# Layer 2's experts: all tokens through all eight, or tokens sorted by expert into tiles of 128

## The chip, the cores and the metric

The kernel runs on one core of a Trainium2 chip. The core has a matrix engine (TensorE, here PE; its weight loads are PEld), a vector engine (VectorE, DVE), an activation engine (ScalarE, ACT), a general engine (GpSimd, POOL) and an engine that only issues transfers (SyncE, SP). They run side by side, each its own instructions in order, and wait for one another through semaphores. Transfers are carried out by 16 DMA engines. The metric is device microseconds for one execution of the whole program; lower is better.

## The reference

2048 tokens of 128 features (two batches of 1024) pass through four layers. Each layer is a feed-forward half step, an attention step and the same feed-forward half step again. The change concerns layer 2, whose feed-forward part is a mixture of eight experts of which each token uses the two with the highest router logits. Its input is the layer norm of x, and half of its output is added to x:

```python
logits = x_flat @ router_w
gate_vals, gate_idx = jax.lax.top_k(logits, TOP_K)             # TOP_K = 2
gate_w = jax.nn.softmax(gate_vals, axis=-1)
gates = jnp.zeros_like(logits).at[jnp.arange(N)[:, None], gate_idx].set(gate_w)
h = jax.nn.gelu(jnp.einsum('nd,edf->enf', x_flat, w1) + b1[:, None, :], approximate=False)
out = jnp.einsum('enf,efd->end', h, w2) + b2[:, None, :]
res = x_flat[None, :, :] + out
mu = jnp.mean(res, axis=-1, keepdims=True)
var = jnp.mean(jnp.square(res - mu), axis=-1, keepdims=True)
normed = (res - mu) * jax.lax.rsqrt(var + LN_EPS)
expert_out = normed * gamma[:, None, :] + beta[:, None, :]
y = jnp.einsum('end,ne->nd', expert_out, gates)
```

Here d = 128 and f = 512 per expert. The reference computes all eight experts for every token; six of the eight gates of a token are zero.

## The kernel before

Everything is float32. `c.x` holds the whole of x in SBUF, as 16 tiles of 128 tokens; four tiles make a chunk q of 512 tokens. The program is written as one stream. Only TensorE's order is taken as written (`manual_schedule` for PE); the other engines' instructions are ordered by a scheduler. Work that prepares the next stage is put into "threads": lists of pieces with `None` between them. `c.tick()` advances the first two threads up to their next `None`, and `c.need(key)` runs the rest of a thread at once. So a piece's place in TensorE's stream depends on how many ticks have passed.

Layer 2's feed-forward part (`l2_ffn`) runs `experts` (L270 to L330) over 4 chunks by 8 experts, 32 steps. In a step `hidden` makes the 512 hidden features of 512 tokens (four products of 512 columns, L284, with GELU and the bias on ACT, L292), then `output` does the step before: b2 by a product with ones (L299) and 16 products of 128 by 128 (L302). `combine` adds the input (L1166), takes the norm's statistics (L1168), and for each pair of experts works out scale and offset on DVE, applies them on ACT (L1183), multiplies by gamma on POOL (L1185) and adds to x on DVE (L1189). There is one tick per step. All of layer 2's weights, 2 MB for each of w1 and w2, are loaded once, before the first use (`l2_weights`).

The preparation of a chunk (`l2_ffn_prep`) is a norm (`norm_pieces`), a turn to feature order (L163), the router's logits (L218), the best two of eight (`top2`), the gates, and the beta term added to x (L267, L269). It takes eleven advances. Layer 1's feed-forward part, which comes before the first of layer 2, finishes chunk q at its iteration 4q + 8 of 21, with one tick per iteration. Layer 2's attention (`l2_attn`) comes between the two feed-forward parts; it handles eight groups (two batches by four head groups) of 16 steps with a tick each, and the last group's output is added to x after the last step. Its first projection (L1234 to L1263) is not interleaved with anything. After the second feed-forward part, layer 3 works on chunks that take 256 tokens from each batch (`places`), so its first needs tokens of both batches.

Of the kernel before, what the change touches and what calls it, by code (L numbers as in the profile page):

```python
# [29 lines left out]
class Ctx:  # L30
# [44 lines left out]
    def advance(self, thread):  # L75
        pieces = thread[1]
        while pieces:
            piece = pieces.popleft()
            if piece is None:
                break  # L80
            piece()
        if not pieces:
            self.threads.remove(thread)

# [89 lines left out]
def norm_pieces(c, r, q, scale=1.0, eps=1e-5, weight=None):  # L174


    def xs(j):
        return c.x[:, 4 * q + j, :]

    def apply():  # L180
        r["xn"] = c.act.tile([P, 4, P], F32, tag="xn", name="xn", bufs=4)
        norm_apply(c, r, xs, r["xn"])

    def turn():
        r["xT"] = by_feature(c, q, r["xn"], weight)

    return [partial(norm_stats, c, r, xs, (scale, eps)), None, None, apply, None, None, turn, None]


def top2(c, v, n):  # L190
# [5 lines left out]
    def largest(x, k):  # L196
        m = c.act.tile([P, 4], F32, tag=f"t2m{k}", name="t2m", bufs=2)
        eq = c.act.tile([P, 4, n], F32, tag=f"t2e{k}", name="t2e", bufs=2)
        f = c.act.tile([P, 4], F32, tag=f"t2f{k}", name="t2f", bufs=2)
        nc.vector.tensor_reduce(m, x, AX.X, ALU.max)  # L200
        nc.vector.tensor_tensor(eq, x, m.unsqueeze(2).to_broadcast([P, 4, n]), ALU.is_equal)
        nc.vector.tensor_tensor(eq, eq, rev, ALU.mult)
        nc.vector.tensor_reduce(f, eq, AX.X, ALU.max)
        nc.vector.tensor_tensor(eq, eq, f.unsqueeze(2).to_broadcast([P, 4, n]), ALU.is_equal)
        return m, eq
# [21 lines left out]
def pair_gates(c, lg, n):  # L227
# [3 lines left out]
    m1, o1, m2, o2 = top2(c, lg, n)  # L231
# [3 lines left out]
    def end():  # L235
        nc.vector.tensor_scalar(m2, m1, -0.25, 0.25, ALU.mult, ALU.add)
        nc.vector.tensor_scalar(m1, m1, 0.25, 0.25, ALU.mult, ALU.add)
        g = c.act.tile([P, 4, n], F32, tag="gates", name="gates", bufs=4)
        nc.vector.tensor_tensor(o1, o1, m1.unsqueeze(2).to_broadcast([P, 4, n]), ALU.mult)
        nc.vector.tensor_tensor(o2, o2, m2.unsqueeze(2).to_broadcast([P, 4, n]), ALU.mult)  # L240
        nc.vector.tensor_add(g, o1, o2)
        return g
# [4 lines left out]
def gate_pieces(c, r, q, router, n, rows, bias=None):  # L247
# [3 lines left out]
    def gates():  # L251
        r["end"] = pair_gates(c, router_logits(c, r, router, n, bias), n)
# [884 lines left out]
def l2_weights(c, pool):  # L1137
    w = {n: c.load(pool, f"l2f_{n}") for n in "router w1 b1 w2 beta".split()}
    w["gamma"] = c.load(pool, "l2f_gamma", rows=P)
    w["b2"] = pool.tile([3, 8 * P], BF16, tag="l2f_b2", name="l2f_b2")  # L1140
    with c.tc.tile_pool(name="parts", bufs=1) as work:
        three_parts(c, work, c.load(work, "l2f_b2", rows=3), w["b2"])
    for n in "wq wkv wo norm gq gk".split():
        w[n] = c.load(pool, f"l2a_{n}")
    return w


def l2_ffn_prep(c, w, rs, q):
    return norm_pieces(c, rs[q], q) + gate_pieces(c, rs[q], q, w["router"], 8, w["beta"])


def l2_ffn(c, w, rs, key, done):
    nc = c.nc
    with c.pool("l2f") as pool:
        two = {}

        def combine(q, e, py):


            k = e % 2  # L1160
            if k == 0:
                two["st"] = pool.tile([P, 4, 2, 6], F32, tag="rst", name="rst", bufs=3)
                two["todo"] = []
            st = two["st"]
            res = pool.tile([P, 4, P], F32, tag="res", name="res", bufs=5)
            nc.vector.tensor_add(res, py, rs[q]["xn"])  # L1166
            for j in range(4):
                nc.vector.bn_stats(st[:, j, k, :], res[:, j, :])  # L1168
            if k:
                mean, var, sc, off = (  # L1170
                    pool.tile([P, 8], F32, tag=n, name=n, bufs=3) for n in ("mean", "var", "sc", "off")
                )
                mean_var(c, mean, var, st)
                inv_sqrt(c, sc, var, 1.0, 1e-6)
                by_tile = lambda a: a.rearrange("p (j e) -> p j e", j=4)
                nc.vector.tensor_tensor(by_tile(sc), by_tile(sc), rs[q]["g"][:, :, e - 1 : e + 1], ALU.mult)
                nc.vector.scalar_tensor_tensor(off, mean, -1.0, sc, ALU.mult, ALU.mult)
                two["sc"], two["off"] = sc, off

            def finish(sc, off):  # L1180
                for j in range(4):
                    a = slice(2 * j + k, 2 * j + k + 1)
                    nc.scalar.activation(res[:, j, :], res[:, j, :], AF.Identity, scale=sc[:, a], bias=off[:, a])  # L1183
                gamma = w["gamma"][:, e * P : (e + 1) * P].unsqueeze(1).to_broadcast([P, 4, P])
                nc.gpsimd.tensor_tensor(res, res, gamma, ALU.mult)  # L1185

            def add():
                xs = c.x[:, 4 * q : 4 * q + 4, :]
                nc.vector.tensor_add(xs, xs, res)  # L1189
                if e == 7:  # L1190
                    done(q)

            two["todo"].append((finish, add))
            if k == 0:
                return []
            (f0, a0), (f1, a1) = two["todo"]
            sc, off = two["sc"], two["off"]
            return [partial(f0, sc, off), partial(f1, sc, off), a0, a1]

        experts(  # L1200
            c, pool, rs, w["w1"], w["w2"], w["b1"], AF.Gelu, 8, 4, combine, key, b2=w["b2"]
        )

# [7 lines left out]
def l2_attn(c, w, rs, key, done):  # L1211
    nc = c.nc
    with c.pool("l2a", 2) as pool:
# [6 lines left out]
        def project(b, f):  # L1220


            raw = pool.tile([P, TB, 2, 4, 64], F32, tag="raw", name="raw", bufs=1)
            tr = pool.tile([P, 2, 2, S], F32, tag="tr", name="tr")
            v = pool.tile([P, TB, 4, 64], F32, tag="v", name="v")
# [136 lines left out]
        for n, (b, f) in enumerate(groups):  # L1362
# [10 lines left out]
            for s in range(16):  # L1373
                k2 = s % 4
                if k2 == 0:
                    u = dict(p=s // 8, q=s // 4 % 2, v=v, aoT=aoT)
# [10 lines left out]
                c.tick()  # L1387
            outs = output(b, f, aoT)
        mix(*before)
        divide(ended)  # L1390
        for piece in outs:
# [26 lines left out]
def l3_ffn_prep(c, w, rs, work, q):  # L1418
# [13 lines left out]
    def apply_first():  # L1432
        r["xn"] = c.act.tile([P, 4, P], F32, tag="xn", name="xn", bufs=4)
# [208 lines left out]
def macaron(ctx: ExitStack, tc: tile.TileContext, dram: dict, out: bass.AP):  # L1642
# [35 lines left out]
    with ExitStack() as s1:  # L1678
# [16 lines left out]
        p2 = ctx.enter_context(c.pool("w2"))  # L1695
        w2 = l2_weights(c, p2)
        l1_ffn(c, w1, r[5], "f", follow("g", partial(l2_ffn_prep, c, w2, r[6])))
    r = [r[6]] + [chunks() for _ in range(4)]
    l2_ffn(c, w2, r[0], "g", follow("h", partial(l2_attn_prep, c, w2, r[1])))
    l2_attn(c, w2, r[1], "h", follow("i", partial(l2_ffn_prep, c, w2, r[2])))  # L1700
# [13 lines left out]
    l2_ffn(c, w2, r[2], "i", both_places)  # L1714
# [108 lines left out]
```

## Time and profile before

| | us |
|---|---|
| median of 3 runs (3280.83 to 3284.17) | 3281.82 |
| time of the profiled execution | 3285.2 |
| its span, first to last instruction | 3283.3 |
| layer 2's first feed-forward part, 1688 to 1940 in the span | 252 |
| layer 2's second feed-forward part, 2716 to 2963 | 247 |
| layer 2's attention with its start, 1940 to 2716 | 776 |

The profile's page gives busy time per engine, the busy share in 40 slices of the span, and the chain of work that ended last. The trace behind it can be asked for groups of instructions by line, for the timeline of a stretch, and for busy times of stretches. A product in float32 is recorded as two matmuls and two weight loads, so the counts are twice those of the code. In the timeline a row is several like instructions in a line: its start, its length, and how many.

### The profile page before, as it was taken

To read this page: it belongs to the slowest core of one execution; us is meant where nothing else is said; L and a number is where in the kernel's file an instruction comes from. 1 tells how busy PE (TensorE), PEld (TensorE's weight loads), DVE (VectorE), ACT (ScalarE), POOL (GpSimd) and SP (SyncE) were. 2 spreads that over 40 slices of the span, in tenths; PEclk is the share of its full clock that TensorE was granted. 3 is DMA by queue.
4 is the path that set the end of the run, shared out by engine and by line. 5 is a ranking of instruction groups with operands and counts; after the bars stand their busy time and mean duration, and the time that the engine had idled before them with its cause. 6 is when DMAs were issued, how large, how long until landed. Compare 5 with 4: busy or idle time off the path is not lost.

```text
span 3283.3 us, 44950 instructions
## 1 busy us (share of the span) xinstructions
PE 2980.2 (91%) x16080; PEld 1683.6 (51%) x16080; DVE 2121.4 (65%) x6759; ACT 1731.0 (53%) x3278; POOL 850.1 (26%) x769
## 2 busy tenths in 40 slices
PE   7999999999898788888789978999989999998989
PEld 5544545454564454444466653343334336666667
DVE  4665566656458588586565567777777755457774
ACT  3355454545333356565245536677756785555443
POOL 0011111111005354454321123544424431111100
PEclk9999999999898589999899998999989999998999
DMA  2000000000000000000100000000000001000000
GB/s 80 1 1 1 1 1 1 1 1 1 25 1 0 1 1 1 1 1 27 58 1 1 1 1 1 1 1 1 0 1 1 1 1 32 1 1 1 1 4 11
DMA packets 14215, 21.80 MB, mean 7 GB/s; under 512 B 5425, under 2 KB 11330, under 8 KB 13350
## 3 DMA queue, kind: packets, MB, share of 16 engines
q1 hardware_dynamic: 8546, 15.90, 1.5%
q10 hardware_dynamic: 5444, 3.01, 0.3%
q8 instruction: 127, 2.08, 0.3%
q14 instruction: 98, 0.80, 0.1%
HBM read 17.86 MB, written 1.05 MB: 6 GB/s over the span
## 4 chain that ended last, share of the span: by engine, by line
PE 74%; DVE 17%; ACT 4%; issue 2%; POOL 2%; DMA 0%; SPq 0%; ACTq 0%; DVEq 0%; POOLq 0%
PE py L302 13%; PE ph L284 12%; PE ps L1304 7%; PE po L1337 6%; PE ps L486 5%; PE po L528 4%; PE ptp L514 4%; PE pr L466 3%; PE po L1065 2%; PE pt L1053 2%; PE pqk L1238 1%; PE pr L556 1%; ACT pe L1031 1%; PE ps L1008 1%; DVE raw L1256 1%
## 5 line engine op out<-in xcount | busy, mean ns | idle before, releaser
L1311 ACT ACTIVATE pe<-ps 128x1024 f32<-128x1024 f32 x256 | 248.8, 1021 | 143.4 <-PE ps L1304 143.4
L1304 PE MATMUL ps<-tr 64*128 64x512 f32 x1024 | 268.4, 645 | 1.6 <-ACT pe L1311 1.6
L292 ACT ACTIVATE hT<-ph,l2f_b 128x512 f32<-128x512 f32 x256 | 162.1, 683 | 185.2 <-PE ph L284 185.2
L499 ACT ACTIVATE pe<-ps,nm 128x512 f32<-128x512 f32 (+3 forms) x384 | 219.6, 578 | 65.1 <-DVE nm L497 61.1
L1337 PE MATMUL po<-pe,v 128*64 128x512 f32 x1024 | 248.4, 606 | 2.3 <-ACT pe L1312 2.3
L1312 ACT ACTIVATE pe<-pe 128x2048 f32<-128x2048 f32 x128 | 244.8, 1913 | 4.1
L302 PE MATMUL py<-l2f_w,hT 128*128 128x128 f32 x2048 | 245.6, 278 | 0.0
L497 DVE TENSOR_REDUCE nm<-ps 128x2 f32<-128x256 f32 (+1 forms) x192 | 182.8, 952 | 95.6 <-PE ps L495 62.3
L302 PEld LDWEIGHTS py<-l2f_w,hT 128*128 128x128 f32 x2048 | 233.5, 192 | 14.5 <-issue 14.3
L347 DVE SCALAR_TENSOR_TENSOR x<-py,gates,x 128x128 f32<-128x128 f32 x448 | 132.7, 344 | 165.7 <-PE py L302 165.6
L284 PE MATMUL ph<-xT,l2f_w 128*128 128x512 f32 x512 | 230.7, 593 | 0.0
L96 ACT COPY pT<-ptp 128x512 f32<-128x512 f32 x192 | 92.0, 479 | 250.8 <-PE ptp L514 250.8
L1185 POOL TENSOR_TENSOR res<-res,l2f_gamma 128x512 f32<-128x512 f32 x64 | 91.0, 1421 | 447.5 <-ACT res L1183 439.5
L486 PE MATMUL ps<-kT,qT 64*128 64x512 f32 (+3 forms) x768 | 177.9, 539 | 30.0 <-ACT pe L499 11.3
L528 PE MATMUL po<-pT,v 128*64 128x512 f32 (+3 forms) x768 | 166.5, 512 | 0.0
L514 PE MATMUL ptp<-ident,pe 128*128 128x128 f32 x1152 | 162.2, 277 | 0.2 <-ACT rb L564 0.2
L1304 PEld LDWEIGHTS ps<-tr 64*128 64x128 f32 x1024 | 92.6, 195 | 129.1 <-issue 90.8
L1337 PEld LDWEIGHTS po<-pe,v 128*64 128x64 f32 x1024 | 62.3, 136 | 176.8 <-issue 150.6
L514 PEld LDWEIGHTS ptp<-ident,pe 128*128 128x128 f32 x1152 | 123.0, 141 | 51.5 <-issue 39.6
L302 PEld LDWEIGHTS py<-l3f_w,hT 128*128 128x128 f32 x1024 | 124.9, 193 | 31.6 <-issue 28.1
L284 PEld LDWEIGHTS ph<-xT,l2f_w 128*128 128x128 f32 x512 | 92.4, 190 | 92.7 <-issue 88.2
L1324 POOL TENSOR_TENSOR acp<-pe 128x1024 f32<-128x1024 f32 x32 | 76.4, 2387 | 220.7 <-ACT pe L1312 158.1
(374 smaller groups left out, 6372.4 us busy)
## 6 DMA issues: line engine op xcount, KB each, us to landing
l2f_w<-in_l2f_w SPq DMA_DIRECT2D x2, 2048.0 KB, 8.4
l3f_w<-in_l3f_w SPq DMA_DIRECT2D x2, 1024.0 KB, 4.9
l0f_W<-in_l0f_W SPq DMA_DIRECT2D x2, 768.0 KB, 4.9
l2a_wkv<-in_l2a_wkv SPq DMA_DIRECT2D x1, 1024.0 KB
x<-in_x SPq DMA_DIRECT2D x2, 256.0 KB
x<-in_x ACTq DMA_DIRECT2D x2, 256.0 KB, 4.5
l0a_wq<-in_l0a_wq SPq DMA_DIRECT2D x1, 512.0 KB
l0a_wqr<-in_l0a_wqr SPq DMA_DIRECT2D x1, 512.0 KB, 7.6
```

Source lines behind the costliest of these rows:

```text
L284: nc.tensor.matmul(ph[:, a, :], lhsT=w1[:, e, (k + a) * P : (k + a + 1) * P], rhs=rs[q]["xT"], start=True, stop=True)
L292: nc.scalar.activation(hT[:, k + a, :], ph[:, a, :], func, bias=bias)
L302: nc.tensor.matmul(py[:, j, :], lhsT=hT[:, k, j * P : (j + 1) * P], rhs=w2[:, e, k, :], start=(k == 0 and b2 is None), stop=(k == hc - 1), ...
L486: nc.tensor.matmul(ps[:, h, :W], lhsT=u["qT"][r, q0 : q0 + P], rhs=u["kT"][r, gk * 512 : gk * 512 + W], start=True, stop=not diag,)
L497: nc.vector.tensor_reduce(nm, ps[:, :, :W], AX.X, ALU.max, negate=True)
L499: nc.scalar.activation(u["pe", n][:, h, i, :W], ps[:, h, :W], AF.Exp, bias=nm[:, h : h + 1], accum_out=u["rs"][:, n, i, h : h + 1],)
L514: nc.tensor.transpose(pt[:, i * P : (i + 1) * P], u["pe", n][:, h, i, j * P : (j + 1) * P], c.ident)
L528: nc.tensor.matmul(u["po", n][r, lo * P :], lhsT=u["v"][:, BLOCKS[n][1] * 4 + j, cols], rhs=u["pT", n, j][h][:, lo * P :], start=(j == 0), ...
L1304: nc.tensor.matmul(ps[:, h, :], lhsT=tr[r, 1, p, k * P : (k + 1) * P], rhs=tr[r, 0, p, q * 512 : (q + 1) * 512], start=True, stop=True,)
L1311: nc.scalar.activation(pe[:, j], ps, AF.Tanh, scale=1.0 / 50.0)
L1312: nc.scalar.activation(pe, pe, AF.Exp, scale=50.0 * 0.125)
L1337: nc.tensor.matmul(u["po"][r, :], lhsT=u["v"][:, k, 2 * u["p"] + h, :], rhs=pe[:, j, h, :], start=(k == 0), stop=(k == TB - 1),)
```

## The change

Layer 2's feed-forward part no longer puts every token through every expert. Tokens are handled in two halves of 1024. For each half:

- The preparation also stores the normed rows in HBM (`xd`), and keeps the two one-hot rows of the chosen experts and the two gates.
- `l2_route` counts, by products of bf16 zeros and ones, how many earlier tokens chose the same expert. Each expert gets whole tiles of 128 places, at most 23 tiles for the 2048 pairs of token and expert. DVE works out each pair's place and each tile's expert; 16 more products invert the table, so that each place knows its token.
- `l2_ffn` runs over the 23 tiles, in groups of four. POOL gathers a tile's rows by an indirect DMA, each engine loads the tile's expert number into a register, SP loads that expert's w1 (256 KB), and the operands w2, b1, b2 and gamma are addressed by the register. There is a tick every second tile. The normed result, without the scale, is stored in HBM with its variance as a 129th column (`yd`).
- `l2_back` gathers, by indirect DMA, the two rows of each token, works out the scale from variance and gate, and adds both to x. It has five advances until x is done.

The first feed-forward part's halves are chunks (0,1) and (2,3), the second's (0,2) and (1,3). In `l2_attn` the last group handles its first 512 queries first and adds their output to x at steps 10 and 11, with two ticks per step from step 10. w2, gamma and b2 are loaded twice, the second time during that group. Buffers of `tr` and `v` lie in two pools, and `xn` has two buffers instead of four, with layer 3's in a pool of its own.

```diff
-def l2_ffn(c, w, rs, key, done):
...
+TILES = 23
+GROUPS = [range(i, min(i + 4, TILES)) for i in range(0, TILES, 4)]
...
+def l2_ffn_prep(c, w, keep, h, a):
...
+    def store():
+        nc.sync.dma_start(out=h["xd"][512 * a : 512 * a + 512, :].rearrange("(j p) d -> p j d", p=P), in_=r["xn"])
+
+    def end():
+        h["ready"] += 1
+        if h["ready"] == 2:
+            c.later(("route", h["name"]), l2_route(c, w, keep, h))
...
+    return [begin] + norm[:i] + [store] + norm[i:] + gates + [end]
...
+def l2_route(c, w, keep, h):
...
+        nc.tensor.matmul(ahead, lhsT=w["before"], rhs=m, start=True, stop=False, skip_group_check=True)
+        for t in range(TB - 1):
+            rhs = m[:, t : t + 1, :].to_broadcast([P, TB - 1 - t, 8])
+            nc.tensor.matmul(
+                ahead[:, t + 1 :, :], lhsT=c.ones16, rhs=rhs, start=False, stop=(t == TB - 2), skip_group_check=True
+            )
...
+    def one_hot_row():
+        r["a"] = tile_([16, P], "a", BF16)
+        nc.vector.tensor_tensor(r["a"], wide(w["iota"], 16), long(r["lo"], P), ALU.is_equal)
+
+    def invert():
+        pt = r["pt"] = c.bank("pt")[:, 0:48]
+        for k in range(16):
+            nc.tensor.matmul(
+                pt, lhsT=r["a"][:, k, :], rhs=r["b"][:, k].rearrange("p a i -> p (a i)"), start=(k == 0), stop=(k == 15)
+            )
...
+    return [pairs, None, count, None, places, None, one_hot, one_hot_row, None, None, invert, None, tokens, None]
...
+def l2_ffn(c, w, we, keep, halves, done):
...
+        def fetch(n):
+
+            h, g = groups[n]
+            xg[n] = keep.tile([P, 4, P], F32, tag="xg", name="xg", bufs=4)
+            for j, i in enumerate(g):
+                at = bass.IndirectOffsetOnAxis(ap=h["tok"][:, i : i + 1], axis=0)
+                nc.gpsimd.indirect_dma_start(xg[n][:, j, :], None, h["xd"], at)
+                e = expert[n, j] = nc.values_load(
+                    h["ex"][0:1, i : i + 1],
...
+                w1[n, j] = pool.tile([P, 512], F32, tag="w1", name="w1", bufs=8)
+                nc.sync.dma_start(
+                    out=w1[n, j], in_=c.dram["l2f_w1"][:, bass.ds(e, 1), :].rearrange("p e f -> p (e f)")
+                )
+
+        def ahead(n, force):
+
+            while fetched[0] < min(n + 3, len(groups)):
+                key = ("route", groups[fetched[0]][0]["name"])
+                if fetched[0] <= n and force:
+                    for a in range(2):
+                        c.need(("half", groups[fetched[0]][0]["qs"][a]))
+                    c.need(key)
+                elif groups[fetched[0]][0]["ready"] < 2 or c.waits(key):
+                    return
+                fetch(fetched[0])
+                fetched[0] += 1
...
+            for a in range(4):
+                nc.scalar.activation(
+                    hT[:, a, :], ph[:, a * P : (a + 1) * P], AF.Gelu, bias=w["b1"][:, bass.ds(e * 4 + a, 1)]
+                )
...
+            nc.vector.tensor_add(res[:, 0:m, :], py[:, 0:m, :], xg[n][:, 0:m, :])
+            for j in range(m):
+                nc.vector.bn_stats(st[:, j, 0, :], res[:, j, :])
+            mean_var(c, mean[:, 0:m], y[:, 0:m, P], st[:, 0:m])
...
+            nc.sync.dma_start(out=rows, in_=y[:, 0:m, :])
+            if g is GROUPS[-1]:
+                c.later(("back", h["name"]), l2_back(c, keep, h, done))
...
+        for k, (n, j) in enumerate((n, j) for n in range(len(groups)) for j in range(len(groups[n][1]))):
+            if j == 0:
+                if n == 0:
+                    ahead(0, True)
+                    turn(0)
+                if n + 1 < len(groups):
+                    ahead(n + 1, True)
+            if j == 2 and n + 1 < len(groups):
+                turn(n + 1)
+            now = (n, j, hidden(k, n, j))
+            if last is not None:
+                output(*last)
+            last = now
+            if k % 2:
+                c.tick()
...
+def l2_back(c, keep, h, done):
...
+                nc.gpsimd.indirect_dma_start(yg[a][:, k, j, :], None, h["yd"], at)
...
+    return [partial(fetch, 0), partial(fetch, 1), None, None, None, partial(add, 0), None, partial(add, 1), None]
...
+                if n + 1 == len(groups) and s >= 10:
+                    c.tick()
+                if n + 1 == len(groups) and s == 9:
+                    for d, piece in zip((10, 11), output(b, f, aoT)[0:2]):
+                        slots[d].append(piece)
...
+    h1, prep1 = halves(1, ((0, 1), (2, 3)))
+    h2, prep2 = halves(2, ((0, 2), (1, 3)))
```

## Prediction

> **What bounds the kernel now.** I read the page first: the busy shares, then the chain of waits, then the two stretches of the change alone.
>
> ```profile
> PE 2980.2 (91%) x16080; PEld 1683.6 (51%) x16080; DVE 2121.4 (65%) x6759; ACT 1731.0 (53%) x3278; POOL 850.1 (26%) x769
> ...
> PE 74%; DVE 17%; ACT 4%; issue 2%; POOL 2%; DMA 0%; SPq 0%; ACTq 0%; DVEq 0%; POOLq 0%
> PE py L302 13%; PE ph L284 12%; PE ps L1304 7%; PE po L1337 6%; PE ps L486 5%; PE po L528 4%; PE ptp L514 4%; PE pr L466 3%; PE po L1065 2%; PE pt L1053 2%; PE pqk L1238 1%; PE pr L556 1%; ACT pe L1031 1%; PE ps L1008 1%; DVE raw L1256 1%
> ```
>
> PE leads, and the two products of the experts head the chain. The stretches of layer 2's feed-forward parts (busy time per engine, granted clock, DMA share, GB/s):
>
> ```profile
> 1688.00:1940.00 252.00, 251.04 (x1388) 171.87 (x1386) 133.23 (x638) 137.52 (x266) 42.48 (x30) 1.00 0.00 1
> 2716.00:2963.00 247.00, 247.00 (x1368) 169.26 (x1368) 129.18 (x642) 136.14 (x267) 42.91 (x30) 1.00 0.01 4
> ```
>
> PE is never idle here, at full clock; every other engine is about half free. What leaves PE's stream shortens the program, until another engine or a wait takes over. One step in the timeline (start, length):
>
> ```profile
> 1700.63 3.60 PE L284 MATMUL ph<-xT,l2f_w 128*128 128x512 f32 x8
> ...
> 1704.16 0.39 PE L299 MATMUL py<-l2f_b,ones 3*128 3x512 bf16 x1
> ...
> 1704.48 3.84 PE L302 MATMUL py<-l2f_w,hT 128*128 128x128 f32 x32
> ```
>
> The next step's L284 in an undisturbed stretch comes 7.52 us later (the chain has L284 at 1827.23 and 1834.75). The 32 records of L302 fill 3.77 us there, 0.118 us for 128 columns. 32 steps are 240.6 us; of the two stretches' 499 us, 499 - 481 = 18 us are preparation, which stays.
>
> **The tile loop.** 46 tiles of 128 replace 32 steps of 512: 5888 rows instead of 16384. The padding to 23 tiles per half is always computed. Per tile on PE: hidden 8 records and output 8 records of 128 columns, each 8 x 0.118 = 0.94; b2 0.15 (the three-row bf16 product L721 starts 0.15 before the next); a quarter of a turn, 0.12 (four turns L163 take 0.47). Together 2.15 us, 92 tiles: **198 us** instead of 481.
>
> Can the others keep up? ACT: four GELUs of 128x128. The trace has this form at 267 ns (copy), 364 (with a bias), 483 (scale and bias); L1183's eight follow at 0.40 each. 4 x 0.40 plus half a 0.59 evacuation per group is 1.7 us, under 2.15. DVE per group of four: add 0.69, statistics 0.87, mean and variance 0.6, four scaled subtractions of about 0.3 (L347 takes 0.34), half an evacuation 0.35: 3.7, or 0.9 per tile. Preparations, two routes and two ways back add about 50 us in a stretch, so some 90 us of DVE beside 99 of PE: it holds, with no room to spare. SP: 256 KB per 2.15 us is 122 GB/s; the two 2 MB loads of before landed in 8.4 us, 250 GB/s. Hidden, with eight buffers.
>
> **Registers.** Nothing in the trace shows a register load. Below: nothing, if each sequencer runs ahead of its engine. Above: one load and some ten address instructions per tile. The sequencer's own row is
>
> ```profile
> L302 PEldq EVENT_SEMAPHORE  x82: 51/51/51, 21.7 to 3274.7; - x82
> ```
>
> so 0.5 us for the ten, and for the load the Trainium skill's price: DMA: Bandwidth & Descriptors, section "Latency and other measured facts", gives a `tensor_load` a floor of about 600 ns. All exposed would be 1.1 x 92 = 101 us. By the row, and with the loads issued three groups ahead, a load costs like a few sequencer steps; I take 0.2 us per tile, **18 us**. No run here shows the load.
>
> **The gathers.** 46 forward gathers of 128 rows (64 KB), plus 16 of the first half's 32 back, are on POOL in each stretch; its 30 multiplications (42 us) go. The trace has no transfer issued by POOL. Below: 0.33 us, SP's price for issuing a 2 MB load:
>
> ```profile
> L50 SPq DMA_DIRECT2D l2f_w<-in_l2f_w x2: 328/328/328, 1536.6 to 1562.0; - x2
> ```
>
> Nearest on POOL, also 64 KB per operand, is L1185 at 1.29 us (median). Against this change speaks SBUF — State Buffer, section "SBUF: two separate sides": POOL's cores write the descriptors of such a transfer through a port they share with DVE, and a DVE instruction in a two-port mode locks them out; its example grows from some 620 ns to 3100. The trace shows the lock from the other side:
>
> ```profile
> 1957.73 1.04 POOL L1247 TENSOR_TENSOR sq<-raw 128x512 f32<-128x512 f32 x1 [1.55 <-DVE raw L1245]
> ...
> 1957.84 0.96 DVE L111 SCALAR_TENSOR_TENSOR nw<-nh,nw 128x4 f32<-128x4 f32 x1
> ```
>
> A DVE operation of 0.16 us lasts 0.96 while POOL works. By the row, 62 x 1.3 = 81 us per stretch, hidden. By the rule, 62 x 3.1 = 192 us, and POOL sets the stretch. I take 1.3: the new loop's long DVE operations read PSUM or are statistics, so few of them should lock.
>
> **The route, four times.** This is the new wait. A half's preparation takes eleven advances. Before the first stretch, chunk 1 finishes at iteration 12 of 0 to 20, so it gets nine; before the second, chunk 2 gets ten (ticks of steps 11 to 15, doubled). So `ahead(0, True)` emits the rest and the whole route at once, directly in PE's stream. The second half of each stretch: ten ticks before tile 20, eleven advances needed, so its route too is emitted in one piece at tile 20. PE then stands between `count` and `invert`. By the rows: 18 small DVE operations at 0.20 to 0.28 (chained L110 to L112 start 0.20 apart) 4.2; three of 384 elements 1.5; one of 2048, twice L1329's 1.26, 2.5; 25 small products at 0.12 (L218: eight in 0.97) 3.0; five handovers 1. **12 us**. The gather follows: 4 x 1.3, 2.0 to land (a 128 KB store to HBM lands in 1.9), turn and evacuation 1.1: 8 us. A start costs 20, **40 for two**. At tile 20 two tiles (4.3 us) lie between the route and the next group's turn: 16, **32 for two**. All of this was covered before: chunk 0 was long ready.
>
> **The clock after a stop.** After the 20 us hole at 2966:
>
> ```profile
> 2984.00:2988.00 4.00, 4.00 (x11) 2.45 (x11) 2.61 (x24) 2.47 (x5) 0.00 (x0) 0.50 0.01 2
> 2988.00:2992.00 4.00, 3.28 (x11) 1.45 (x10) 3.60 (x22) 3.05 (x4) 0.00 (x0) 0.89 0.00 0
> ```
>
> Some 4.5 us at half clock: 2.3 us lost per stop, **9 us** for four.
>
> **The way back.** The last group's store in a half is written behind the w1 loads of group 9, and these wait on SP for the buffers of group 7, until about tile 31. POOL's 16 back gathers wait for that store, with group 10's gathers behind them: 31 tiles + 2 us + 21 us is tile 42, where group 10's turn is due at tile 37. If the scheduler keeps this order PE loses about 11 us, and the next stage's preparation as much; if it moves the store forward, nothing. I take 12 per stretch, **24 us**.
>
> **Hidden or small.** The second load of w2, gamma and b2 (2.5 MB, some 12 us) lies beside twelve attention steps of 5.5 us. The start of attention gains: PE waited there 8.9 us for DVE, which was in the last combine; its scale now lies in the way back. I take **-6**. xd's stores and the buffer moves: nothing, long before their use.
>
> **Sum**: 198 + 18 (preparation) + 18 + 40 + 32 + 9 + 24 - 6 = 333 us instead of 499: -166. The profiled execution took 3285.2 (span 3283.3, 1.9 around it), so 3119; the median of the runs is 3.4 lower: **3116 us**.
>
> **Rivals.**
> - *The routes are hidden* (0.15): DVE reaches their parts early, and store and gathers are reordered. Starts 12 each, tile 20 at 6, no way back, registers free, cold clock 4: -16 - 20 - 24 - 18 - 5 = -83, 3033. For it: DVE is half free. Against: `count` stands behind the previous stage's products in PE's fixed order.
> - *POOL sets the loop* at the rule's 3.1 us (0.12): a stretch is 20 + 192 = 212, the two 424 + 3 instead of 499: 3210. For it: the 0.96 above; against: the kind of DVE work.
> - *Slower* (0.07): the price of one gather alone. Two stretches of 20 + 62c, plus 3, reach 499 at c = 3.7 us; above, POOL decides. At 4.5 us: 601, +102, 3384. For it: each of 128 rows is its own descriptor, and no row shows that price; against: POOL does a whole 128x512 operation in 1.3.
> - *No change* (0.02): these losses just eat the gain. That the change does less than it says is excluded: the tile count is fixed in the code.
>
> The likeliest, at 0.64, lies between 3050 and 3185 (registers, way back and starts at either end). The range for 8 in 10 takes most of both neighbours: **3035 to 3215**. A measurement of this kernel can tell 0.2% (6.6 us) from no change. Faster 0.91, same 0.02, slower 0.07.
>
> **What would show it.** Right: both stretches near 165 us; a tile's products 2.2 to 2.4 us apart; four holes in PE of 12 to 20 us, each ending at `invert` or at a gathered tile's turn; POOL's instruction near 1.3 us. Wrong: tiles 3 us or more apart, with PE waiting for a gather (POOL) or for GELU (ACT's registers); a gather above 3.7 us; no holes at tile 20; or a loss in attention or layer 3 larger than 15 us, which I have not priced.

## The result and the profile after

The changed kernel takes 3230.93 us (median of 4 runs, 3221.69 to 3233.3), against 3281.32 us (3278.9 to 3284.17) for the kernel before: a ratio of 0.9841, 95% interval 0.982 to 0.9862. The forecast was 3116 us, with a range of 3035 to 3215. The direction is right, but the gain is some 50 us instead of 166. The profiled executions (3285.2 and 3221.7 us) differ by 63.5, which is 13 us more than the medians do; what follows accounts for the 63.5. The busy shares and the chain of waits, from the page of the changed kernel:

```profile
PE 2753.7 (86%) x15214; PEld 1578.9 (49%) x15214; DVE 2048.4 (64%) x6398; ACT 1585.2 (49%) x3148; POOL 909.6 (28%) x861
...
PE 62%; DVE 20%; ACT 5%; issue 4%; another core or an unknown queue 3%; POOL 3%; DMA 2%; ACTq 1%; SPq 0%; DVEq 0%; POOLq 0%
```

PE lost 226 us of work, but the program lost only 63: waits took the rest. "Another core or an unknown queue" was not in the chain before. It is the profile's name for a wait whose end it can give to no instruction (in the rows below such a wait is called "remote"), and it turns out to be the main story. The two tile loops, and the parts around them, in busy time per engine (columns: stretch, length, PE, PEld, DVE, ACT, POOL, granted clock, DMA share, GB/s):

```profile
1689.00:1707.70 18.70, 3.38 (x36) 2.15 (x34) 9.05 (x36) 2.05 (x4) 6.84 (x7) 0.55 0.52 162
1707.70:1891.50 183.80, 132.36 (x906) 117.37 (x907) 67.01 (x334) 63.63 (x201) 52.00 (x55) 0.83 0.32 91
1891.50:1941.40 49.90, 21.58 (x81) 14.48 (x80) 33.39 (x95) 0.00 (x0) 23.84 (x24) 0.69 0.09 25
...
2713.80:2899.10 185.30, 134.16 (x907) 119.35 (x908) 70.34 (x360) 68.25 (x212) 54.95 (x64) 0.83 0.35 92
```

Where PE was busy all the time at full clock, it now stands still for 51 us of 184, and DVE, ACT and POOL are each busy for less than 40%. Nothing is saturated, so something makes PE wait. Cut at the same events (the stretch's first hidden product, its last output product, attention's last score product), the two profiled executions compare like this:

| us | before | after | difference |
|---|---|---|---|
| to the first hidden product of stretch 1 | 1688.0 | 1707.7 | +19.7 |
| stretch 1, first hidden to last output product | 249.1 | 183.8 | -65.3 |
| attention with its start, to the last score product | 763.3 | 788.6 | +25.3 |
| to the first hidden product of stretch 2 | 15.6 | 33.6 | +18.0 |
| stretch 2 | 247.4 | 185.3 | -62.1 |
| the rest | 320.0 | 320.9 | +0.9 |

The two holes at the starts were forecast (20 each). The loops (a stretch from its first hidden to its last output product) were forecast at 150 each and take 184 and 185. Attention was forecast 6 us shorter and is 25 longer.

**Where the loops stop.** The timeline of the first stop, in stretch 1 (start, length, instruction, in brackets the idle time before it and what ended it):

```profile
1711.19 2.08 PE L1375 MATMUL ph<-xgT,w 128*128 128x128 f32 x8 [1.46 <-ACT hT L1383]
1711.47 0.95 POOL L1331 DMA_INDIRECT xg<-xd,r_tok  x1 [0.30 <-issue]
...
1713.41 1.86 PE L1402 MATMUL py<-l2f_w,hT 128*128 x8
...
1717.73 0.95 POOL L1331 DMA_INDIRECT xg<-xd,r_tok  x1 [0.30 <-issue]
1718.67 3.49 SPq L1340 DMA_DIRECT2D w<-in_l2f_w  x2
1718.74 1.50 ACT L1383 ACTIVATE hT<-ph,l2f_b 128x128 f32<-128x128 f32 x4 [7.61 <-remote]
```

The hidden products of tile 1 end at 1713.3. GELU waits for nothing else that the trace shows, and elsewhere starts 0.1 us after them. Here it starts at 1718.74, and the w1 load that waits for the same products is issued at 1718.67. Meanwhile POOL writes gathers one after the other. The semaphore updates in the trace say that PE had done its work and that only the news of it was late: the four transposes recorded at 1715.1 to 1715.7 count up PE's semaphore at 1721.62, 1721.65, 1721.68 and 1721.72, 0.03 us apart, where each takes 0.11 us to compute. Call the time between the end of a tile's hidden products and its GELU, where it is above 0.6 us, late release. Over the 46 tiles of a stretch it sums to 69 us in the first and 71 us in the second, and the same tiles are hit in both: 1, 2, 6, 10, 21, 22 and 25 to 28. Tiles 26 to 28 lie beside the 16 gathers of the first half's way back, with 14 us at tile 27.

### The profile page after: what moved, and what is told of

Same layout as the page of the kernel before. It is cut to its first block, busy times and chain, and to the rows that moved or that the text cites. A ratio compares the mean times of both kernels' runs of the same rounds, so it can differ in the third digit from the quotient of the medians.

```text
span 3219.9 us, 44643 instructions
## 1 busy us (share of the span) xinstructions
PE 2753.7 (86%) x15214; PEld 1578.9 (49%) x15214; DVE 2048.4 (64%) x6398; ACT 1585.2 (49%) x3148; POOL 909.6 (28%) x861
## 3 DMA queue, kind: packets, MB, share of 16 engines
q0 software_dynamic: 4992, 10.27, 1.6%
## 4 chain that ended last, share of the span: by engine, by line
PE 62%; DVE 20%; ACT 5%; issue 4%; another core or an unknown queue 3%; POOL 3%; DMA 2%; ACTq 1%; SPq 0%; DVEq 0%; POOLq 0%
PE ps L1586 6%; PE po L1619 5%; PE ph L290 5%; PE ps L492 5%; PE py L308 5%; PE po L534 4%; PE ptp L520 4%; PE pr L472 3%; PE ph L1375 3%; PE po L1071 2%; PE pt L1059 2%; PE py L1402 2%; PE pr L562 1%; PE pqk L1520 1%
## 5 line engine op out<-in xcount | busy, mean ns | idle before, releaser
L503 DVE TENSOR_REDUCE nm<-ps 128x2 f32<-128x256 f32 (+1 forms) x192 | 182.7, 951 | 95.0 <-PE ps L501 61.3
L1383 ACT ACTIVATE hT<-ph,l2f_b 128x128 f32<-128x128 f32 x368 | 110.6, 368 | 213.5 <-remote 85.3
L492 PE MATMUL ps<-kT,qT 64*128 64x512 f32 (+3 forms) x768 | 177.4, 538 | 30.1 <-ACT pe L505 11.4
L1375 PE MATMUL ph<-xgT,w 128*128 128x128 f32 x736 | 118.6, 312 | 51.0 <-ACT hT L1383 36.5
L1331 POOL DMA_INDIRECT xg<-xd,r_tok x92 | 87.4, 950 | 243.7 <-issue 97.2
L1402 PE MATMUL py<-l2f_w,hT 128*128 x736 | 121.3, 313 | 39.2 <-ACT hT L1383 31.9
L1619 PEld LDWEIGHTS po<-pe,v 128*64 128x64 f32 x1024 | 62.5, 137 | 177.4 <-issue 152.5
L1529 POOL TENSOR_TENSOR sq<-raw 128x512 f32<-128x512 f32 x64 | 89.5, 1398 | 162.1 <-DVE raw L1527 107.1
L1045 POOL TENSOR_SCALAR pe<-pe,rs 128x256 f32<-128x256 f32 (+7 forms) x128 | 94.7, 753 | 141.6 <-DVE rs L1042 76.7
```

The lines of the kernel that those rows point to most:

```text
L492: nc.tensor.matmul(ps[:, h, :W], lhsT=u["qT"][r, q0 : q0 + P], rhs=u["kT"][r, gk * 512 : gk * 512 + W], start=True, stop=not diag,)
L503: nc.vector.tensor_reduce(nm, ps[:, :, :W], AX.X, ALU.max, negate=True)
L1375: nc.tensor.matmul(ph[:, a * P : (a + 1) * P], lhsT=wt[:, a * P : (a + 1) * P], rhs=xT[n][:, j * P : (j + 1) * P], start=True, stop=True,)
L1402: nc.tensor.matmul(py, lhsT=hT[:, a, :], rhs=we["w2"][:, bass.ds(e, 1), a, :].rearrange("p e d -> p (e d)"), start=False, stop=(a == 3), s ...
L1619: nc.tensor.matmul(u["po"][r, :], lhsT=u["v"][:, k, 2 * u["p"] + h, :], rhs=pe[:, j, h, :], start=(k == 0), stop=(k == TB - 1),)
```

## The experiments

Theory A: while POOL writes indirect gathers, the end of PE's products is seen late by all who wait for it. Rival B: the stops come from w1's stream, the registers or ACT's order, and only coincide with the gathers. A single execution of one program can lie 10 us from another of the same program, and the traces show such a difference before layer 2: in the changed kernel, e2, e4, e7, e8 and e12, whose code is the same up to there, the first hidden product comes at 1706.5 to 1716.3 us. The kernel before, run beside the experiments, took 3282 to 3293 us. So the lengths of the two loops are the finer measure. They are those of one profiled execution each; the time is a single run, but for e10 to e12, where it is the median of 4, 4 and 6 runs (their profiled executions took 3197.8, 3195.5 and 3190.9 us):

| run | loop 1 | loop 2 | time, us |
|---|---|---|---|
| changed kernel, profiled | 183.8 | 185.3 | 3221.7 |
| e1 forward gathers replaced | 159.0 | 162.1 | 3167.1 |
| e2 way back replaced | 166.0 | 162.3 | 3160.5 |
| e3 both replaced | 139.8 | 140.7 | 3114.6 |
| e4 way back spread | 183.9 | 180.4 | 3256.5 |
| e5 plain transfers from POOL | 140.0 | 144.8 | 3102.5 |
| e6 constant experts | 177.4 | 177.1 | 3198.0 |
| e7 a PSUM tile per tile | 173.5 | 175.2 | 3200.0 |
| e8 an advance per tile | 169.5 | 187.9 | 3201.3 |
| e9 rows in order | 184.8 | 181.5 | 3229.5 |
| e10 combined | 159.8 | 182.2 | 3197.4 |
| e11 and squares on ACT | 163.3 | 180.9 | 3192.0 |
| e12 without layer 1's | 163.3 | 182.7 | 3175.4 |
| e13 half the rows | 191.9 | 187.3 | 3236.8 |

### e1 to e3: no indirect transfer forward, backward, or at all

```diff
-                at = bass.IndirectOffsetOnAxis(ap=h["tok"][:, i : i + 1], axis=0)
-                nc.gpsimd.indirect_dma_start(xg[n][:, j, :], None, h["xd"], at)
+                t = i % TB
+                nc.sync.dma_start(out=xg[n][:, j, :], in_=h["xd"][t * P : (t + 1) * P, :])
...
-                at = bass.IndirectOffsetOnAxis(ap=h["si"][:, col : col + 1], axis=0)
-                nc.gpsimd.indirect_dma_start(yg[a][:, k, j, :], None, h["yd"], at)
+                nc.sync.dma_start(out=yg[a][:, k, j, :], in_=h["yd"][col * P : (col + 1) * P, :])
```

e1 has the first half of this diff, e2 the second, e3 both.

> Leaves out the sorted order of the rows: each tile of 128 rows is read from xd in plain order by a transfer of SP instead of POOL's indirect gather; the way back still gathers. Theory A (while POOL writes gathers back to back, the end of PE's products reaches ACT, DVE and SP late): the stops after tiles 1, 2, 6, 21 and 22 of a stretch go (some 17 us per stretch), those at tiles 25 to 28 (some 20 us), where POOL writes the way back, stay; with shorter starts about 3170 us. Rival B (the stops come from the stream of w1, the register loads or the order of ACT, and only coincide with the gathers): all stops stay, the starts get some 4 us shorter each, about 3205 us.

> Leaves out the order of the way back: the 64 gathers from yd become plain transfers of SP; the forward gathers stay. A: the stops at tiles 25 to 28 go (20 us per stretch), those at tiles 1, 2, 6, 21, 22 stay; the start of attention, where POOL's squares stand between 16 gathers, gets some 20 us shorter: about 3160 us. B: all stops stay, only the start of attention gets shorter: about 3200 us.

> Leaves out both orders: no indirect DMA is left; routing, registers, w1 loads and tiles stay as they are. A: no stop of PE's release is left, a stretch falls from 202 to about 160 us, attention starts 20 us earlier: about 3110 us. B: stretches of some 195 us, about 3185 us.

Measured: 3167.1, 3160.5 and 3114.6 us, each within 5 us of what A gives and far from B. The stops divide as A says: in e1 only those beside the way back are left (at tiles 29 and 30 there), in e2 only the forward ones, in e3 none (1.3 and 2.0 us of late release in a whole stretch). Of the two loops' 369.1 us, the way back alone (e1 against e3) holds 40.6 us, the forward gathers alone (e2 against e3) 47.8; together 88.4, and e3 is 88.6 shorter than the changed kernel. Routing, registers, w1's stream and tiles are untouched in e3, so B falls. PE's work is the same, and it runs at a granted clock of 0.91 instead of 0.83 (the columns as above):

```profile
1710.20:1849.90 139.70, 121.60 (x906) 108.06 (x907) 71.89 (x365) 64.59 (x201) 0.00 (x0) 0.91 0.44 121
```

The group row of GELU says it in one line each (busy, mean ns, idle before and what ended it); from the page of e3:

```profile
L1383 ACT ACTIVATE hT<-ph,l2f_b 128x128 f32<-128x128 f32 x368 | 111.4, 367 | 131.5 <-PE ph L1375 124.7
```

and from that of the changed kernel:

```profile
L1383 ACT ACTIVATE hT<-ph,l2f_b 128x128 f32<-128x128 f32 x368 | 110.6, 368 | 213.5 <-remote 85.3
```

The same GELUs, as long as before; 85 us of waits without a name are gone.

### e4: the way back in small portions

```diff
-    return [partial(fetch, 0), partial(fetch, 1), None, None, None, partial(add, 0), None, partial(add, 1), None]
+    spread = [s for a in range(2) for j in range(4) for s in (partial(fetch, a, j), None)]
+    return spread[:8] + spread[8:] + [None, partial(add, 0), None, partial(add, 1), None]
```

> Computes all. The way back's 16 gathers per half are put two to an advance (every second tile) instead of eight to an advance. If A holds and it is the burst that does it: the stops at tiles 25 to 28 shrink from 20 to some 5 us per stretch, about 3190 us. If each gather costs PE the same wherever it stands: the stops spread over more tiles and the time stays at 3220 to 3230 us. If B holds: no change of the stops.

Measured: 3256.5 us, a miss on every side. The edit spread the pieces over the program's advances, but it did not take the burst apart: in the trace, POOL still writes 12 of the 16 gathers back to back in stretch 1, 1.25 us from one to the next (1825.5 to 1839.2 us), and only the last four later (1848.7 to 1852.4). From tile 25 on, the late release falls from 36 to 23 us in stretch 1 and from 41 to 27 in stretch 2. So this run does not settle whether a gather that stands alone holds PE as long as one in a burst. The loops gain 0 and 5 us, and what comes after stretch 2 takes 359.3 us instead of 320.9. There the last four gathers of the first half come at 2848 to 2852 us instead of 2842 at the latest, 10 us later; what makes the rest of the 38 us is not shown. (That the longer list of pieces keeps layer 3's preparation from advancing is a guess.)

### e5: the same rows, moved by plain transfers of POOL

```diff
-                nc.gpsimd.indirect_dma_start(xg[n][:, j, :], None, h["xd"], at)
+                nc.gpsimd.dma_start(out=xg[n][:, j, :], in_=h["xd"][t * P : (t + 1) * P, :])
```

and likewise for `yg`.

> Leaves out both orders, as e3 does, but the rows are moved by plain transfers that POOL issues, as many and as large as the gathers. A1 (whatever transfer POOL writes the descriptors of holds PE's release back): the stops stay, 3200 to 3230 us. A2 (only the indirect form does, by its 128 single rows): hardly a stop is left, 3115 to 3140 us.

Measured: 3102.5 us, 12 us below the range of A2 and far from that of A1. POOL's software queue carries the same 4992 packets and 10.27 MB as in the changed kernel, and GELU starts at once beside it. From the timeline of e5:

```profile
1806.81 1.16 PE L1375 MATMUL ph<-xgT,w 128*128 128x128 f32 x8 [0.26 <-ACT hT L1383]
1807.10 2.11 POOL L1464 DMA_DIRECT2D yg<-yd  x4 [4.36 <-DMA yd<-y]
...
1808.08 1.36 ACT L1383 ACTIVATE hT<-ph,l2f_b 128x128 f32<-128x128 f32 x4 [1.31 <-PE ph L1375]
```

Four transfers in 2.1 us, the products end in the midst of them, and GELU follows 0.1 us later. So neither the traffic, nor the queue, nor POOL as the issuer holds the release. Nor does POOL's being busy: in the kernel before it multiplies for 42 us in each stretch, and PE never stands. It is the indirect form.

### e9 and e13: what of the indirect form?

```diff
-        nc.vector.scalar_tensor_tensor(h["tok"], r["pt"][:, 24:48], float(P), low, ALU.mult, ALU.add)
+        nc.vector.tensor_scalar(h["tok"], w["iota"][:, 0:24], 0.0, w["pidx"], ALU.mult, ALU.add)
```

> Leaves out the sorted order: the forward gathers keep their instruction and their table, but the table holds the rows 0 to 127 in order, for every tile. Theory F (the indirect instruction itself holds PE's release back, whatever it fetches): the stops stay, 3215 to 3235 us. Rival (the scattered rows do it, on the side of the transfers): the forward stops go as in e1, about 3175 us.

```diff
-                at = bass.IndirectOffsetOnAxis(ap=h["tok"][:, i : i + 1], axis=0)
-                nc.gpsimd.indirect_dma_start(xg[n][:, j, :], None, h["xd"], at)
+                at = bass.IndirectOffsetOnAxis(ap=h["tok"][0:64, i : i + 1], axis=0)
+                nc.gpsimd.indirect_dma_start(xg[n][0:64, j, :], None, h["xd"], at)
+                nc.sync.dma_start(out=xg[n][64:P, j, :], in_=h["xd"][t * P + 64 : (t + 1) * P, :])
```

> Leaves out the sorted order of half the rows: each forward gather fetches 64 rows, the other 64 of the tile come by a plain transfer of SP; as many indirect instructions as before, half the rows. If the hold goes with the rows written out (128 per instruction): POOL's instruction falls from 0.95 to about 0.5 us and the forward stops to about half, 3195 to 3210 us. If it goes with the instruction, whatever its length: 0.95 us and the stops stay, 3215 to 3235 us.

Measured: 3229.5 us for e9, in the range of theory F, and 3236.8 us for e13, 2 us above the range of "the instruction, whatever its length". The tiles to compare are 6 and 10, whose gathers stand at the same place in all three kernels. There the release is 2.8 to 2.9 and 1.1 us late in the changed kernel, the same in e9, though every gather fetches the same 128 rows in order, and 3.3 and 1.3 to 1.5 us in e13. Elsewhere e9 moved the gathers: its table needs no route, so the first ones lie before the stretch (1677 to 1696 us) and tiles 1 and 2 are free, while stops appear at tiles 14 and 18. Its late release sums to 40 and 54 us instead of 69 and 71, so that its loops are as long as those of the changed kernel is in part chance. In e13 the gather's rows, from the trace (ns min/median/max):

```profile
L1332 POOL DMA_INDIRECT xg<-xd,r_tok x92: 897/906/1107, 1707.6 to 2875.6; - x92
```

Half the rows cost 0.91 us instead of 0.95, and the late release sums to 74 us in each stretch (69 and 71 in the changed kernel). It is not the same at every tile: at 21 and 22 together it is 9.4 and 4.8 us instead of 17.1 and 12.7, and at the way back, whose gathers are unchanged, it is longer. Rows and bytes were halved, but not packets: POOL's queue carries 4992 of them in both kernels (7.25 instead of 10.27 MB). So an indirect gather is priced by the piece here, on POOL and, at tiles 6 and 10, on PE's side. What within the instruction keeps PE's semaphore from counting stays open.

### e6: constant expert numbers

```diff
-                e = expert[n, j] = nc.values_load(
...
+                e = expert[n, j] = i % 8
```

> Leaves out the choice of the expert: tile i uses expert i mod 8, a constant, so that no engine loads a register and no address is worked out; the gathers stay. The prediction's term (0.2 us per tile): 18 us less, about 3205 us. Rival 1 (the sequencers run ahead, registers cost nothing): 3218 to 3230 us. Rival 2 (it is the register steps in PE's stream that, beside the gathers, hold its release back): the stops go, about 3140 us.

Measured: 3198.0 us, loops 14.6 us shorter together. The prediction's term (18) holds in size, rival 2 falls: the stops stay (62 and 46 us of late release). They moved, though, so the 14.6 us are not the registers alone. Where the cost lies was not as thought. 8.6 us of it are at tile 20, where twelve register loads of the next three groups follow each other in PE's own stream, behind the forced route: the distance from tile 19 to tile 20 falls from 15.9 to 11.6 us. One load takes PE 0.31 us.

### e7: a PSUM tile for each tile's hidden products

```diff
-            if k % 2 == 0:
-                two["ph"] = c.pair("ph")
-            ph = two["ph"][:, k % 2, :]
+            ph = c.pair("ph")[:, 0, :]
```

> Computes all. Each tile's hidden products get a PSUM tile of their own, instead of one for two tiles. Theory P (the second tile of a pair waits until GELU has read the first, because both lie in one PSUM tile: 1.47 us after its products against 1.1 us of the other products in between, 0.37 us per pair): 46 pairs, 17 us less, about 3205 us. Rival (the pace of undisturbed tiles is set elsewhere, by DVE or by the preparation in between): no change, 3220 to 3230 us.

Measured: 3200.0 us, loops 20.4 us shorter together, against 17 by theory P. The late release is longer than in the changed kernel (77 and 94 us), so the saving comes from elsewhere: in 21 tiles of each loop that no gather disturbs (4, 5, 8, 9, 11 to 18, 32 and 37 to 44) the distances to the next tile sum to 52.2 and 52.8 us instead of 57.9 and 58.2. PE's idle time before its hidden products falls to 21.6 us, of which 2.4 are ended by GELU; in the changed kernel it was

```profile
L1375 PE MATMUL ph<-xgT,w 128*128 128x128 f32 x736 | 118.6, 312 | 51.0 <-ACT hT L1383 36.5
```

In the changed kernel two neighbouring tiles shared one PSUM tile, and the second tile's products waited for GELU to read the first tile's half. It is a wait that the prediction did not see, since it is not in the instructions' costs but in what they share.

### e8: an advance at every tile

```diff
-            if k % 2:
-                c.tick()
+            c.tick()
```

> Computes all. The preparation advances at every tile instead of at every second. Theory R (at tile 20 PE waits 14 to 16 us because the second half's route is written out there in one piece): the route is done before tile 20, the hole goes, some 28 us less, about 3195 us. Rival (DVE has no room, or the gathers' stops only move): 3215 to 3230 us.

Measured: 3201.3 us, nearer to theory R than to the rival. The hole at tile 20 goes (15.9 to 5.7 us from tile to tile in both stretches). Loop 1 gains 14 us; loop 2 gains nothing, since layer 3's preparation moves into it (946 records of products instead of 907), and the rest of the program is 9.7 us shorter instead.

### e10 to e12: together

e10 is e7, e8 and more advances ahead of the stretches. e11 adds the squares on ACT, and e12 drops the advance in layer 1.

```diff
+            if t >= 12:
+                c.tick()
...
                 if n + 1 == len(groups) and s >= 10:
                     c.tick()
+                    c.tick()
...
+                if b == 0 and f == 0:
+                    nc.scalar.activation(sq, raw[:, j], AF.Square)
+                else:
+                    nc.gpsimd.tensor_mul(sq, raw[:, j], raw[:, j])
```

> Computes all: a PSUM tile for each tile's hidden products (e7, -22), an advance at every tile (e8, -20), and two advances an iteration in layer 1's last nine iterations and three in the last six steps of attention, so that the first half's route is written out earlier (a part of the two start holes of 18 us, at most -20). If the three add up: 3160 to 3180 us. If DVE has no room before the starts, or PE waits there for the route in the previous stage instead: 3180 to 3200 us.

> Computes all: e10, and the squares of attention's first projection on ACT, which is idle there, instead of on POOL, where they stand between the 16 gathers of the way back. If these squares lengthen the start of attention (50 us, against 37 to 41 with no gather): some 10 us less than e10. If the way back's gathers themselves set it: the same as e10 within 3 us.

> Computes all: e11 without the second advance in layer 1 (there PE waited for the route between layer 1's own products, and the first tile came 15 to 18 us later). If that is the whole loss: e11's 3192 less 16, about 3176 us. If the earlier route was also what shortened the first stretch: about 3190 us.

Measured against the kernel before, which ran beside each: e10 0.973 (0.9709 to 0.975), e11 0.9705 (0.9684 to 0.9726), e12 0.9674 (0.9657 to 0.969), with medians of 3197.4, 3192.0 and 3175.4 us. In e10 the parts don't add up: its time is the one forecast for that case. With the second advance in layer 1, the first hidden product comes at 1726 us in e10 and 1723 in e11; without it, at 1716 in e12. That layer 1's own products wait there for the route's was argued, and no run shows it alone. The squares on ACT shorten the start of attention from 50.3 to 45.9 us: POOL's turn was part of it. e12 computes everything and beats both kernels: its interval lies below that of the changed kernel (0.982 to 0.9862). Its median is what was forecast for it, but the intervals of e10, e11 and e12 overlap each with the next, so these two single steps are not shown by the times. e12's runs spread from 3172 to 3191 us. The gathers are still in it, and so are the stops, 79 us of late release in each stretch.

## Why the prediction was right and wrong

The step that failed is the cover of the gathers: "62 x 1.3 = 81 us per stretch, hidden". It holds for POOL and not for PE, and the gathers cost 88 us in the two loops, where the sum had 24, for another reason. By the steps of the sum, 333 us forecast for what was 499 before:

- **Right: the starts.** Two holes of 20 us forecast, 19.7 and 18.0 measured between the two profiles. Within the trace of the changed kernel, `count` stands at 1689.5, the table is ready at 1698.4, and the first products start at 1707.7: 9 us for the route and 9 for the gather, forecast at 12 and 8.
- **Right in kind: the routes at tile 20.** Four holes, each as described; 16 forecast for each of these two, 13.5 measured (15.9 us from tile 19 to tile 20, less 2.4 for an undisturbed tile). The inversion starts 7.6 us after the counting, and 4.1 us of what follows are PE's register loads, which the sum had put in another term.
- **Right: registers.** 18 forecast, 14.6 by e6. The load's price by the Trainium skill (DMA: Bandwidth & Descriptors, section "Latency and other measured facts", a floor of about 600 ns) is not what this trace shows. The load's rows (ns min/median/max):

```profile
L1332 SPq TENSOR_LOAD <-r_exi x92: 231/271/699, 1692.9 to 2870.2; - x92
...
L1332 PEldq TENSOR_LOAD <-r_exi x92: 295/306/1016, 1697.3 to 2855.6; - x92
```

- **Right by luck: the gather's own price**, 1.3 us forecast, 0.95 and 0.30 to the next one measured. The row it was taken from, L1185, works on 128x512 float32, 256 KB per operand and not 64, and is no transfer. The lock by DVE that the rule warns of (SBUF — State Buffer, section "SBUF: two separate sides") does not show in the changed kernel: none of the 92 forward gathers takes more than 1.165 us. In e9 one takes 1.62 us, beside DVE additions of two SBUF operands of 1.22 us each, so the rule is not refuted; its case is rare here.
- **Wrong, and the largest: the gathers, hidden.** They are hidden on POOL, which is busy 52 of 184 us. They are not hidden from PE, whose finished products are announced 1 to 14 us late beside them. The forward gathers, entered at nothing, hold 47.8 us in the two loops, by e2 and e3.
- **Wrong in mechanism: the way back, 24 us.** A late store, at about tile 31, and a queue behind it were expected. The gathers start at 1821.0 us, beside tile 26, and what cost was the same hold, 40.6 us in the loops by e1 and e3.
- **Missing: the pair of tiles in one PSUM tile**, 20.4 us by e7. The tile's work itself was well priced: e3's loops are 280.5 us; less registers 14.6, the routes at tile 20 of 27 and the pair's 20.4 they leave 218.5, against 198 + 18 + 9 = 225 us forecast for tiles, preparation and cold clock. The savings of e6 and e7 are taken as additive here, which was not tried.
- **Wrong: attention, -6 us; it became +25.** The start, forecast shorter, is 3.9 us longer (49.9 instead of 46.0): POOL's squares stand between the gathers of the second half's way back, which the sum had left out. Without gathers there, in e2, e3 and e5, the start takes 37 to 41 us, about the 40 forecast:

```profile
1901.76 0.94 POOL L1465 DMA_INDIRECT yg<-yd,r_si  x1 [0.30 <-issue]
1902.71 1.06 POOL L1529 TENSOR_TENSOR sq<-raw 128x512 f32<-128x512 f32 x1
1903.93 0.99 POOL L1465 DMA_INDIRECT yg<-yd,r_si  x1 [0.16 <-issue]
```

The last group, entered under "hidden or small", takes 83.9 us instead of 65.7. In it PE, never idle there before, stands 8.9 us; the rest is work moved in and a clock of 0.92 instead of 1.00. The groups of PE's products in that stretch name the waits (idle time in the last columns):

```profile
L1631 PE MATMUL pn<-acc,ones 128*64 128x512 f32 x16 | 5.1, 722 | 3.0 <-DVE acc L1615 3.0
L222 PE MATMUL pl<-l2f_router,xT 128*128 128x8 f32 x8 | 1.9, 364 | 4.3 <-ACT xT L99 4.3
```

The first stands behind the second load's splitting of b2 into three parts, which DVE does in between (0.7 to 3.4 us an operation); the second is the preparation that the doubled advances brought there. No experiment took these apart.

Of the 103 us between the forecast gain and the profile's, the hold makes 64 (88 less the 24 entered for the way back), attention 31 and the pair 20; starts, routes, registers and tiles give 17 back. Some 3 us lie in the rest of the program and in where the stretches are cut (252 and 247 us in the forecast, 249.1 and 247.4 here). The rival that ends nearest, POOL setting the loop (3210), has the time but not the mechanism, since POOL is idle for over 70% of the loops. Among the signs of being wrong that were named beforehand, two came true: tiles 3 us and more apart with PE waiting for GELU (but not for the reason given there, ACT's registers), and a loss above 15 us in attention.

## What to carry to other kernels

When a change brings in an instruction that no trace shows, pricing the instruction is half the work: ask also what it does to engines that don't wait for it, and keep a case for that. The waits that the profile called remote or unknown, in this program with one core, were releases that came late; where you see such waits, replace the suspect by an equal transfer of another form before believing in bandwidth. Check in the trace, too, that an edit moved what it was meant to move: e4's did not take the burst apart. Two tiles in one buffer can chain engines as firmly as a data dependency, as in e7.

## What the hardware showed that was not expected

- An indirect gather on POOL delays the release of PE's products, by 1 to 14 us at a time in the changed kernel and about 44 us per stretch of 46 tiles (184 against 140), while a plain transfer of the same bytes on the same queue does not (140 and 145). In the same bursts the releases of ACT come through at once: at 1827.10 GELU ends and at 1827.15 PE starts, in the midst of 16 gathers:

```profile
1826.01 0.94 POOL L1465 DMA_INDIRECT yg<-yd,r_si  x1 [0.30 <-issue]
1826.22 0.88 ACT L1383 ACTIVATE hT<-ph,l2f_b 128x128 f32<-128x128 f32 x3 [0.39 <-issue]
1827.15 2.08 PE L1375 MATMUL ph<-xgT,w 128*128 128x128 f32 x8 [4.29 <-ACT hT L1383]
1827.26 0.95 POOL L1465 DMA_INDIRECT yg<-yd,r_si  x1 [0.31 <-issue]
```

- The delay outlasts POOL's instruction. The first burst's last gather ends at 1718.68, and the products of tile 2, done at 1716.60, are announced at 1721.81. The 16 gathers of the way back end at 1840.71, and the GELU of tile 27 starts at 1843.11.
- It goes by instructions and not by rows: 64 rows take POOL 0.91 us, 128 rows 0.95, and at tiles 6 and 10 both hold PE about equally (3.3 and 1.3 to 1.5 us; 2.8 to 2.9 and 1.1). A plain transfer of POOL takes 0.53 us.
- A stop costs PE more than its length: the granted clock is 0.83 in both loops of the changed kernel, 0.91 in those of e3, and was 1.00 before. The same 906 records of products keep PE busy for 132.4 us in loop 1 of the changed kernel and for 121.6 in e3's.
